# Attention stage of a four-layer graph network: a head's exponential placed behind a scaling of mid-head, its row load asked for earlier, copies of weighted sums in the buffers of x

## Chip, cores and metric

The kernel runs on one core of one Trainium2 chip. The metric is the device time in microseconds (us) of one execution; several runs of a kernel are given by their median. One further execution was taken with the hardware profiler, and all stretches below are us from the start of its span.

## The reference

Four graph layers are applied one after the other to `x` (2708 nodes by 512 features) with one symmetric 0/1 adjacency. Each layer adds its result to `x` and begins with a layer norm and a ReLU. The change lies in the third, the attention layer with 8 heads of 64 features:

```
h    = relu(layernorm(x))
Wh   = einsum('nd,hdo->hno', h, W)             # per head, 2708 x 64
e    = leaky_relu(f1[:, :, None] + f2[:, None, :], 0.2)
e    = where(adj > 0, e, -9e15)
att  = softmax(e, axis=-1)
x    = x + elu(einsum('hnm,hmo->hno', att, Wh))  # heads side by side
```

## The kernel before

**Tiling.** The 2708 nodes are cut into 22 chunks of 126 rows (the last has 62). The attention is worked as ten units: head 0 in two halves of its columns, heads 1 to 6 whole (2708 columns), head 7 in two halves. A unit has 22 steps, one for each chunk of neighbours, so there are 220 steps in one loop (L1219 to L1234). Steps are written here as m = 0 to 21 within a unit; a prime (0', 1') marks steps of the following unit.

**One step.** `make` (L876, instruction L883, VectorE) builds the weight tile `t` from the exponentiated row `rb` of the head, the column factor `ec` and the adjacency `vT`; `t` has 4 buffers. `scale` (L866, ScalarE) makes the stationary operand `whs` from `wh` (L872), and in steps that are not "by side" also its part for the sums (L874); `whs` has 4 buffers. `compare` (L894, instruction L901, ScalarE) makes a Sigmoid tile `b` (2 buffers) in the 13 "by side" steps of heads 1 to 6 (m mod 5 is 1, 3 or 4). `multiply` (L1074, matmuls L1066, TensorE) accumulates the weighted sums `av` and, in the other steps, `sums`; `multiply_sides` adds the sums of a by-side step from `b`, one step later. The loop traces `scale` and `make` three steps ahead of `multiply`, and `compare` one step ahead.

**PSUM.** There are 8 buffers of one bank each. A whole head holds five: three for `av`, two for `sums`. So the `sums` of the next head's step 0 need buffers that `evict` (L1099, copies L1105 on ScalarE into `out`, then stores on SP's queue) has to free first. `out` shares the tag `t` of pool `common` with 3 buffers.

**Row of a head.** `load_row1` (L835, DMA on SP's queue, 1.3 MB) broadcasts a head's row into `rb` (2 buffers), and `exp_row` (L845, instruction L847) takes its exponential in place on ScalarE. A buffer of `rb` is free when the last `make` of the head two before is done.

**Counting stage.** In head 0's steps 11 to 37, `mask` (L1133, copies L1138 on ScalarE) casts quarters of the adjacency into the 5 buffers of `x`, and `count_neighbors` (L1140, matmuls L1150) sums them. Four copies serve one count. Later, `load3` loads the first chunks of `x` for the work that follows the attention; these tiles use the same 5 buffers.

**What sets the order.** Each engine runs its instructions in one fixed order. It is not the order of the trace above but that of the framework's scheduler, which may place an instruction earlier as soon as its buffer is free by its own count. The dictionary `plan` (filled by `behind`) only says at which step a function is traced; `tc.issue_after(ins)` makes what is traced in its block follow `ins` on the same engine. In the scheduled program of this kernel, the exponential of head h+1 stands at the border between heads h-1 and h, directly behind the Sigmoid of step 21 and ahead of the border's copies, although it is traced in step 8 of head h; the one of head 1 runs in the middle of head 0's first half (880.93 us).

Of the kernel before, what the change touches and what calls it, by code (L numbers as in the profile page):

```python
# [8 lines left out]
F32 = mybir.dt.float32  # L9
# [5 lines left out]
AF = mybir.ActivationFunctionType  # L15
# [5 lines left out]
P = 128  # L21
# [9 lines left out]
SLOPE2 = 0.2  # L31
# [13 lines left out]
def fast_layers(  # L45
# [36 lines left out]
    nc = tc.nc  # L82
    N, D = x_in.shape
    H, _, O = w2.shape
# [7 lines left out]
    def rows(c):  # L92
        return min(R, N - c * R)
# [17 lines left out]
    XBUFS = 5  # L111
# [11 lines left out]
    common = ctx.enter_context(tc.tile_pool(name="common", bufs=2))  # L123
# [293 lines left out]
    with ExitStack() as ring_ctx:  # L417
# [30 lines left out]
        with tc.tile_pool(name="l0", bufs=2) as wk:  # L448
            units = [(g, m) for g in range(len(groups)) for m in range(NC)]
            tiles, uppers, acc, sums, xs = {}, {}, {}, {}, {}  # L450
# [352 lines left out]
    units = [(h, 0, N) for h in range(H)]  # L803
# [5 lines left out]
    def by_side(u, m):  # L809
        return 0 < units[u][0] < H - 1 and m in BY_SIDE  # L810
# [19 lines left out]
    one6 = at.tile([R, S], F32, name="one6")  # L830
    nc.gpsimd.memset(one6, 0.0)
    nc.gpsimd.memset(one6[:, 6:7], 1.0)
    row, weight, wh, whs, acc, sides, made = {}, {}, {}, {}, {}, {}, []

    def load_row1(h, lo, hi):  # L835

# [7 lines left out]

    def exp_row(h, lo, hi):  # L845
        t = row[h][:, lo:hi]
        nc.scalar.activation(t, t, AF.Exp, scale=1.0 - SLOPE2)  # L847


    GROUP = 3  # L850
# [15 lines left out]
    def scale(s):  # L866

        u, m = steps[s]
        h, q = units[u][0], rows(m)
        t = at.tile([R, O + S], F32, name="whs", bufs=4)  # L870
        by = ef[:q, m, h : h + 1]
        nc.scalar.activation(t[:q, :O], wh.pop((u, m))[:q], AF.Copy, scale=by)  # L872
        if not by_side(u, m):
            nc.scalar.activation(t[:q, O:], one6[:q], AF.Copy, scale=by)  # L874
        whs[s] = t

    def make(s):
        u, m = steps[s]
        h, lo, hi = units[u]
        q = rows(m)  # L880
        g, k = where[m]
        t = at.tile([R, N], F32, name="t2", bufs=TILES)
        ins = nc.vector.scalar_tensor_tensor(  # L883
            t[:q, : hi - lo],
            row[h][:q, lo:hi],
            ec[:q, m, h : h + 1],
            vT[g][:q, k, lo:hi],
            op0=ALU.max,
            op1=ALU.mult,
        )  # L890
        weight[s] = t
        made.append(ins.ins)
# [74 lines left out]
    def rows2(c):  # L967
        if c < LATE:
            row2(c)
        if c == EARLY - 1:  # L970
            load_row1(*units[0])

        if c == LATE:
            exps2(slice(0, EARLY))
            exp_row(*units[0])
            load_wh(0)
            load_wh(GROUP)
        if LATE < c <= LATE + 3:
            scale(len(made))
            make(len(made))  # L980
# [71 lines left out]
    def pieces(w):  # L1052

        k = -(-w // 512)
        cuts = [round(i * w / k) for i in range(k + 1)]
        return list(zip(cuts, cuts[1:]))

    def sizes_of(u):
        _, lo, hi = units[u]
        return (hi - lo) // 2, (hi - lo) // 4  # L1060
# [38 lines left out]
    def evict(u, which):  # L1099
        h, lo, hi = units[u]  # L1100
        size = sizes_of(u)[which]
        dst, height, step = (sumT, 7, S) if which else (avT, O, O)
        for p, (a, b) in zip(acc[u][which], pieces(size)):
            t = common.tile([P, D], F32, name="out", tag="t", bufs=3)
            nc.scalar.copy(t[:, : b - a], p[:, : b - a])  # L1105
            for j in range(P // step):
                nc.sync.dma_start(
                    dst[h * height : (h + 1) * height, lo + j * size + a : lo + j * size + b],
                    t[j * step : j * step + height, : b - a],
                )  # L1110
# [68 lines left out]
    def behind(s, fn, *args):  # L1179
        plan.setdefault(s, []).append((fn, args))  # L1180
# [3 lines left out]
    behind(4, exps2, slice(EARLY, NC))  # L1184
    behind(5, load_row1, *units[1])
    behind(6, exp_row, *units[1])
    behind(9, split)
    behind(30, load_l3_weights)
    behind(30, exp_nodes)
    for u in range(2, len(units)):  # L1190
        if units[u][1] == 0:
            s = max(1, u - 1) * NC
            behind(s + 4, load_row1, units[u][0], 0, N)
            behind(s + 8, exp_row, units[u][0], 0, N)
    for u in range(len(units)):
        behind((u + 1) * NC - 1, evict, u, 0)
        behind(min((u + 1) * NC, len(steps) - 1), evict, u, 1)
# [21 lines left out]
    for s in range(len(steps)):  # L1219
        if s + 6 < len(steps) and (s + 6) % NC % GROUP == 0:  # L1220
            load_wh(s + 6)
        if s + 3 < len(steps):
            scale(s + 3)
            make(s + 3)
        if s + 1 < len(steps):
            compare(s + 1)
        multiply(s)
        multiply_sides(s - 1)
        for fn, args in plan.pop(s, ()):
            if fn in (load_l3_weights, exp_nodes, split):  # L1230
                with tc.issue_after(made[s]):
                    fn(*args)
            else:
                fn(*args)  # L1234
# [698 lines left out]
def kernel(tc: tile.TileContext, *args: bass.AP):  # L1933

    nc = tc.nc
    with tc.tile_pool(name="verdict", bufs=1) as pool:
        verdict = pool.tile([1, 1], I32, name="verdict")
        fast_layers(tc, *args, verdict)
        odd = nc.values_load(verdict[0:1, 0:1], min_val=0, max_val=P + 1)
        with tc.If(odd > 0):  # L1940
            general_layers(tc, *args)
# [32 lines left out]
```

## Time and profile before

| what | value |
|---|---|
| median of 3 runs | 1825.34 us (1822.24 to 1826.04) |
| profiled execution, its own time | 1825.62 us |
| its span | 1823.8 us, so 1.8 us lie around the span |
| TensorE busy (share of span) | 1785.4 us (98%) |
| VectorE busy | 1308.3 us (72%) |
| ScalarE busy | 796.6 us (44%) |
| attention, first `av` to last `av` matmul | 856.6 to 1416 us |

How to read it: a matmul's end is modelled and matmuls overlap, so a busy TensorE does not say that it is TensorE that sets the pace. For that one has to look at one stage and see which engine has no idle time there and which engine the others wait for. The numbers after a line's bar are the busy time and the mean of one instruction in ns; what follows the second bar is idle time in front of them and what ended most of it. In a timeline the square bracket gives the idle time ahead of the line and what ended it.

### The profile page before, as it was taken

What the parts mean: (1) busy time and instruction counts of PE and PEld (TensorE: products, weight loads), DVE (VectorE), ACT (ScalarE), POOL (GpSimd) and SP (SyncE); (2) the same over time, 40 slices, a digit from 0 to 9 for tenths busy, and PEclk for the clock granted to TensorE, in tenths of its full rate; (3) what the DMA queues carried; (4) which work ended last, traced back from release to release, by engine and by line L of the source; (5) the groups of instructions that cost most, each with busy time, mean ns of one, the idle gap of its engine ahead of it and who ended that gap; (6) DMA issues with size and microseconds to landing.
All of it is one profiled execution on the core that took longest, in us unless ns stands there. A gap on an engine that the chain in (4) does not pass through costs nothing.

```text
span 1823.8 us, 30715 instructions
## 1 busy us (share of the span) xinstructions
PE 1785.4 (98%) x11884; PEld 1041.1 (57%) x11884; DVE 1308.3 (72%) x1836; ACT 796.6 (44%) x1542; POOL 245.2 (13%) x241
## 2 busy tenths in 40 slices
PE   9999999999999999999999999999999999999998
PEld 4456777654448887644544344334444445488776
DVE  4942998855446655788999999999989777533334
ACT  2632777731210000156896676776744566400000
POOL 0101323301110211266000000000000222100000
PEclk9999999999999999999999999999999999999999
DMA  7632666635462211353231121121012444313221
GB/s 247 193 112 67 204 209 199 193 80 115 116 143 58 71 57 46 94 149 104 73 89 35 33 61 41 29 61 53 15 36 53 130 139 131 95 34 109 82 68 45
DMA packets 165553, 176.62 MB, mean 97 GB/s; under 512 B 94830, under 2 KB 115792, under 8 KB 164516
## 3 DMA queue, kind: packets, MB, share of 16 engines
q1 hardware_dynamic: 143170, 131.47, 26.3%
q10 hardware_dynamic: 18484, 33.28, 5.3%
q0 software_dynamic: 3744, 9.82, 1.6%
q8 instruction: 95, 1.56, 0.4%
q14 instruction: 60, 0.49, 0.1%
HBM read 111.35 MB, written 55.15 MB: 91 GB/s over the span
## 4 chain that ended last, share of the span: by engine, by line
PE 77%; DVE 11%; DMA 5%; issue 4%; POOL 1%; ACT 1%; SPq 0%; ACTq 0%; DVEq 0%; POOLq 0%
PE acc L368 32%; PE av L1066 16%; PE nb_ps L184 6%; PE sums L1066 6%; DVE t L883 5%; PE self_ps L184 4%; PE wh_ps L184 3%; PE line_ps L184 2%; PE h_ps L184 2%; DVE cum L494 2%; PE fused_ps L312 2%; PE hT_ps L212 1%; DMA x<-x 1%; DMA rb<-rT 1%; DMA packed<-two 1%
## 5 line engine op out<-in xcount | busy, mean ns | idle before, releaser
L883 DVE SCALAR_TENSOR_TENSOR t<-rb,ec,vT 126x2708 f32<-126x2708 f32 (+2 forms) x220 | 532.4, 2469 | 20.6 <-PE sums L1066 10.9
L368 PE MATMUL acc<-halves,kt 126*126 126x512 f32 x1848 | 435.5, 395 | 3.7 <-DVE kt L741 2.1
L1066 PE MATMUL av<-t,whs 126*32 126x451 f32 (+3 forms) x4576 | 436.5, 515 | 0.6 <-DVE ln_mv L191 0.6
L368 PEld LDWEIGHTS acc<-halves,kt 126*126 126x126 f32 x1848 | 342.6, 186 | 93.1 <-DVE kt L741 6.5
L1066 PEld LDWEIGHTS av<-t,whs 126*32 126x32 f32 (+1 forms) x4576 | 160.2, 110 | 206.9 <-issue 181.7
L368 PE MATMUL acc<-halves,ar 126*126 126x512 f32 x924 | 235.4, 408 | 4.3 <-ACT ar L488 2.4
L901 ACT ACTIVATE b<-t,eb 126x2708 bf16<-126x2708 f32 (+1 forms) x78 | 199.0, 2551 | 21.2 <-DVE t L883 21.0
L368 PEld LDWEIGHTS acc<-halves,ar 126*126 126x126 f32 x924 | 171.0, 189 | 55.4 <-issue 8.1
L193 ACT ACTIVATE ln_rs<-ln_mv,eps 126x1 f32<-126x1 f32 x88 | 25.6, 293 | 341.1 <-DMA x<-x 199.2
L741 DVE SCALAR_TENSOR_TENSOR kt<-lastr,index,vT 126x504 fp32r<-126x504 int16 (+3 forms) x154 | 110.4, 728 | 80.9 <-PE acc L368 80.7
L1291 DVE CAST kt<-vT 126x504 fp32r<-126x504 uint8 (+3 forms) x154 | 55.9, 365 | 138.2 <-PE acc L368 138.2
L1066 PE MATMUL sums<-t,whs 126*32 126x338 f32 (+5 forms) x1568 | 140.5, 451 | 5.1 <-ACT out L1105 5.1
L872 ACT ACTIVATE whs<-wh,ef 126x64 f32<-126x64 f32 x220 | 76.6, 350 | 130.1 <-PE sums L1066 73.7
L1033 POOL TENSOR_SCALAR z<-y 126x512 f32<-126x512 f32 x22 | 44.0, 2000 | 664.8 <-DVE y L1026 656.0
L494 DVE TENSOR_TENSOR_SCAN cum<-ai,deg 126x504 int16<-126x504 int32 (+2 forms) x110 | 128.4, 1180 | 0.6 <-DMA ai<-in_adj 0.6
L522 ACT ACTIVATE cum<-cum,limit 126x504 int16<-126x504 int16 (+3 forms) x132 | 88.1, 667 | 59.9 <-DVE deg L502 58.9
L1066 PEld LDWEIGHTS sums<-t,whs 126*32 126x32 f32 (+1 forms) x1568 | 55.3, 109 | 73.1 <-issue 40.7
L189 DVE BATCH_NORM_STATS2 ln_st<-x 126x6 f32<-126x512 f32 x88 | 60.2, 685 | 45.7 <-DMA x<-x 30.8
L184 PE MATMUL h_ps<-w0s,hT 128*126 128x512 f32 x176 | 81.2, 605 | 4.7 <-ACT hT L214 3.5
L184 PE MATMUL nb_ps<-wfn,hT 128*126 128x512 f32 x176 | 80.7, 602 | 3.1 <-ACT hT L214 3.1
L184 PE MATMUL wh_ps<-w2s,hT 128*126 128x512 f32 (+1 forms) x176 | 79.4, 593 | 0.0
L184 PE MATMUL nb_ps<-wn,hT 128*126 128x512 f32 x176 | 79.2, 592 | 0.0
(182 smaller groups left out, 1870.6 us busy)
## 6 DMA issues: line engine op xcount, KB each, us to landing
x<-x SPq DMA_DIRECT2D x105, 252.0 KB
x<-x ACTq DMA_DIRECT2D x84, 252.0 KB
ai<-in_adj SPq DMA_DIRECT2D x84, 249.0 KB
x<-in_x SPq DMA_DIRECT2D x42, 252.0 KB
rb<-rT SPq DMA_DIRECT2D x7, 1332.8 KB
wh<-whd SPq DMA_DIRECT2D x70, 94.5 KB
packed<-two POOLq DMA_DIRECT2D x44, 124.5 KB, 4.5
whd<-wh SPq DMA_DIRECT2D x21, 252.0 KB
```

The costliest lines, as they stand in the source:

```text
L184: nc.tensor.matmul(po[:n], lhsT[:, f, :n], w[:, f, :], start=(f == 0), stop=(f == NF - 1))
L189: nc.vector.bn_stats(st[:n], xc[:n])
L368: nc.tensor.matmul(acc[:R], weight[:, k * R : (k + 1) * R], parts[:, i, :], start=(m == 0 and i == 0), stop=(m == NC - 1),)
L494: nc.vector.tensor_tensor_scan(cum[:n, :gw], ai[:n, :gw], ai[:n, :gw], 0.0 if g == 0 else deg[:n, m : m + 1], op0=ALU.add, op1=ALU.max,)
L522: nc.scalar.activation(cum[:n, :gw], cum[:n, :gw], AF.Sign, bias=limit[:n], scale=-1.0, accum_out=signs[:n, m, g : g + 1],)
L741: nc.vector.scalar_tensor_tensor(by_chunk(kt, cs), lastr[:, cs[0] * R : (cs[-1] + 1) * R].rearrange("p (c r) -> p c r", r=R), index[:R, m ...
L872: nc.scalar.activation(t[:q, :O], wh.pop((u, m))[:q], AF.Copy, scale=by)
L883: ins = nc.vector.scalar_tensor_tensor(t[:q, : hi - lo], row[h][:q, lo:hi], ec[:q, m, h : h + 1], vT[g][:q, k, lo:hi], op0=ALU.max, op1=AL ...
L901: nc.scalar.activation(b[:q, : hi - lo], weight[s][:q, : hi - lo], AF.Sigmoid, bias=eb[:q, m, h : h + 1], scale=STEEP,)
L1033: nc.gpsimd.tensor_scalar(z, y, 0.0, None, op0=ALU.min)
L1066: nc.tensor.matmul(p[j * S : (j + 1) * S, : b - a], lhsT, rhs[:, part * size + a : part * size + b], start=(s % NC == 0), stop=(s % NC == ...
L1291: nc.vector.tensor_copy(by_chunk(kt, cs), pattern(m, cs))
```

## The change

Three edits, all in the attention. First, `scale` records its instruction in a new list `scaled`, and `exp_row` is traced in a block that puts the exponential behind the last recorded scaling; it is traced in step 9 of a unit instead of 8. At that point the loop has traced `scale` up to step 12 of the unit, so it is the scaling of step 12 that the exponential now follows. Second, the row load is traced in step 2 instead of step 4. Third, copies of `av` of the six whole heads take the 5 buffers of `x` instead of the 3 of `t`; copies of `sums`, and those of the half heads, stay where they were.

```diff
     def exp_row(h, lo, hi):
         t = row[h][:, lo:hi]
-        nc.scalar.activation(t, t, AF.Exp, scale=1.0 - SLOPE2)
+        with tc.issue_after(scaled[-1]) if scaled else ExitStack():
+            nc.scalar.activation(t, t, AF.Exp, scale=1.0 - SLOPE2)
...
-        nc.scalar.activation(t[:q, :O], wh.pop((u, m))[:q], AF.Copy, scale=by)
+        ins = nc.scalar.activation(t[:q, :O], wh.pop((u, m))[:q], AF.Copy, scale=by)
         if not by_side(u, m):
             nc.scalar.activation(t[:q, O:], one6[:q], AF.Copy, scale=by)
         whs[s] = t
+        scaled.append(ins.ins)
...
         for p, (a, b) in zip(acc[u][which], pieces(size)):
-            t = common.tile([P, D], F32, name="out", tag="t", bufs=3)
+            tag, bufs = ("x", XBUFS) if (lo, hi) == (0, N) and which == 0 else ("t", 3)
+            t = common.tile([P, D], F32, name="out", tag=tag, bufs=bufs)
             nc.scalar.copy(t[:, : b - a], p[:, : b - a])
...
             s = max(1, u - 1) * NC
-            behind(s + 4, load_row1, units[u][0], 0, N)
-            behind(s + 8, exp_row, units[u][0], 0, N)
+            behind(s + 2, load_row1, units[u][0], 0, N)
+            behind(s + 9, exp_row, units[u][0], 0, N)
```

In the scheduled order this gives: on ScalarE the exponential of every head from 1 to 7 stands directly behind the scaling of step 12 of the unit ahead of it (for head 1, in head 0's second half, ahead of the four mask copies of the eleventh count). At a border, the Sigmoid of step 1' now stands ahead of the copies of `av`. On SP's queue the row loads keep their places among the other transfers; five loads of `x` move from the end of the counting stage (924 us) to behind the stores of head 6 (about 1341 us). The orders of TensorE, VectorE and GpSimd are the same.

More of the change, by code (lines that the diff above doesn't have):

```diff
@@ L832, in fast_layers @@
     nc.gpsimd.memset(one6[:, 6:7], 1.0)
-    row, weight, wh, whs, acc, sides, made = {}, {}, {}, {}, {}, {}, []
+    row, weight, wh, whs, acc, sides, made, scaled = {}, {}, {}, {}, {}, {}, [], []
     def load_row1(h, lo, hi):
```

## Prediction

> **What bounds the kernel now.** I read the page's busy shares first (TensorE 98%, which decides nothing), then the wait table for 750 to 1330 us, then VectorE alone in order of time over the attention, and last ScalarE and TensorE around the head borders. VectorE's timeline says what sets the pace in heads 1 to 6:
>
> ```profile
> 929.91 80.19 DVE L883 SCALAR_TENSOR_TENSOR t<-rb,ec,vT 126x1324 f32<-126x1324 f32 x28 [0.61 <-PE sums L1066]
> 1010.88 3.04 DVE L883 SCALAR_TENSOR_TENSOR t<-rb,ec,vT 126x2708 f32<-126x2708 f32 x1 [0.78 <-PE sums L1066]
> 1015.67 3.04 DVE L883 SCALAR_TENSOR_TENSOR t<-rb,ec,vT 126x2708 f32<-126x2708 f32 x1 [1.75 <-PE av L1066]
> 1019.03 253.81 DVE L883 SCALAR_TENSOR_TENSOR t<-rb,ec,vT 126x2708 f32<-126x2708 f32 x86 [0.31 <-PE sums L1066]
> 1273.88 3.04 DVE L883 SCALAR_TENSOR_TENSOR t<-rb,ec,vT 126x2708 f32<-126x2708 f32 x1 [1.04 <-PE sums L1066]
> 1277.43 53.39 DVE L883 SCALAR_TENSOR_TENSOR t<-rb,ec,vT 126x2708 f32<-126x2708 f32 x19 [0.51 <-ACT b L901]
> ```
>
> The columns are start, duration, instruction, and in brackets the idle time ahead of it. VectorE runs 80 us and 254 us without a gap, 253.81/86 = 2.95 us for one weight tile. TensorE needs less: the chain of waits shows 14.55 us for five steps (1024.09 to 1038.64), 2.91 us each. So a whole head costs 22 x 2.95 = 65 us of VectorE, and whatever leaves VectorE idle there is lost. It is idle at two borders, 0.78 + 1.75 + 0.31 = 2.84 us at heads 1/2 and 1.04 + 0.51 = 1.55 us at heads 5/6: **4.4 us in all**. The borders themselves, all engines in order of time:
>
> ```profile
> 998.43 2.55 ACT L901 ACTIVATE b<-t,eb 62x2708 bf16<-62x2708 f32 x1 [1.86 <-DVE t L883]
> ...
> 1001.00 1.28 ACT L847 ACT_TABLE_LOAD   x1
> ...
> 1004.95 2.46 ACT L847 ACTIVATE rb<-rb 126x2708 f32<-126x2708 f32 x1 [2.67 <-DMA rb<-rT]
> ...
> 1007.77 1.38 ACT L1105 COPY out<-av 128x451 f32<-128x451 f32 x3
> ...
> 1008.33 2.48 PE L1066 MATMUL sums<-t,whs 126*32 126x338 f32 x16 [3.41 <-ACT out L1105]
> ```
>
> ScalarE finishes the last Sigmoid, loads a table, waits 2.67 us for the row's transfer, takes the exponential, and only then copies `av`; TensorE idles 3.41 us for the freed bank. Head 0 is otherwise: there VectorE waits about 0.36 us on TensorE every second step, so TensorE sets the pace, and ScalarE has no gap between 880.93 and 927.06 us:
>
> ```profile
> 915.89 0.36 ACT L872 ACTIVATE whs<-wh,ef 126x64 f32<-126x64 f32 x1
> 916.14 0.32 ACT L874 ACTIVATE whs<-one,ef 126x32 f32<-126x32 f32 x1
> 916.35 0.76 ACT L1138 CAST x<-vT 126x677 bf16<-126x677 uint8 x1
> ...
> 917.46 2.08 ACT L1138 CAST x<-vT 126x677 bf16<-126x677 uint8 x3
> ```
>
> These are the scaling of step 12 and the four mask copies of the eleventh count. They end at 919.54 us, and TensorE's count starts at 920.17 us: 0.63 us to spare.
>
> [...] copies of banks that were long full wait behind an exponential that waits for a DMA. [...] the table of stretches grants 0.95 of the clock in 1004.5 to 1070 and 1.00 in the four neighbours, and the 16 `sums` matmuls at 1008.33 took 2.48 us where the same 16 took 1.36 at other borders. [...] at 1008.2 to 1010.7 copy, scaling, load and Sigmoid follow each other within 0.1 us.
>
> **The change part by part.**
>
> *Exponential out of the borders (gain).* At heads 1/2 call T the end of the last weight tile of head 1 (998.3). Now ScalarE has there: Sigmoid of step 21 to T+2.7, a pair of scalings to T+3.3, the Sigmoid of step 1', whose tile comes at T + 2 x 2.95 = T+5.9, to T+8.45, then the first copy (0.46) to T+8.9. TensorE wants the bank at about T+6.3 (1004.6 before) and starts at T+9.0 instead of T+10.0: it still waits, 2.7 us for 3.4. But VectorE needs that step's tile back only for the tile of step 4', at T + 4 x 2.95 = T+11.8. The `sums` now end at T+10.4 (1.36 us), before at T+12.5 (2.48 us at half clock). So VectorE doesn't wait: 2.84 us saved. At heads 5/6 the same holds and the 2.88 us wait for the row is gone: 1.55 us. At the other borders VectorE had no gap, nothing to gain. Sum **-4.4 us**.
>
> *Exponential in mid-head (nothing in heads 1 to 6).* Call V the end of the tile of step 9. ScalarE: Sigmoid 9 to V+2.55, scalings of step 12 to V+3.2, table and exponential (1.28 + 2.46) to V+6.9, scaling of 13 to V+7.25, table to V+8.55, Sigmoid 11 to V+11.1. TensorE wants that Sigmoid after step 12, at V + 8.85 + 3.42 = V+12.3, VectorE wants tile 11 back at V+14.75. What covers the 5 us are ScalarE's own waits for TensorE (67.8 us of `whs` waits in 933 to 1420). If that cover were short by more than 1.2 us, Sigmoid 11 would be late next.
>
> *Exponential of head 1 (loss).* It goes between the two scalings at 915.89 and the mask copies at 916.35: exponential to 918.8, two copies (0.69 each) to 920.2, a scaling pair to 920.7, two copies to 922.1, count at 922.2 instead of 920.17. All of TensorE is held behind the count, VectorE's four tiles are full, so its takeover at 929.9 moves by the same **+2.0 us**. Queued behind on ScalarE are the scalings of steps 13 and 14, ready at 920.7 and 922.3, wanted at 922.1 and 924.1 even without the delay; they fit. Bounds: 0 if ScalarE is ahead by then, because the old place at 880.93 is empty (it gained at most 0.11 us a pair of steps since, so I allow 0.4); 2.4 if not even the 0.63 of spare is there.
>
> *Row loads, SP's queue.* Their places among SP's transfers don't change, because they wait for the buffer of the head before last; step 2 for step 4 is worth 0. The exponential now comes some 30 us after the load is issued, for a transfer of 6.3 to 8.0 us, so its 8.9 us of DMA waits go.
>
> *Buffers of x.* The copies of `sums` waited 0.4 us once for a store; worth 0 to -0.4, taken as 0. The five moved loads of `x` (252 KB each, 0.31 us of issue each) stand among the `wh` loads of head 7. Those are issued when a buffer of three groups comes free, some 7 steps of 1.75 us = 12 us ahead of use; the row of 1333 KB took 6.3 to 8.0 us, so 1260 KB hold a `wh` back by about that: hidden. Wanted at 1402 us, issued by 1345. 0, at worst +1.
>
> Sum: -4.4 + 2.0 = **-2.4 us** on the profiled execution's 1825.62, which is 0.28 over the median: 1823.2, I say **1823.3**.
>
> **Rivals.** *The exponential in the counting stage costs nothing* (ScalarE ahead of the masks): 1825.6 - 4.4 - 0.4 = 1820.8. For it: that stage loses a 2.46 us exponential earlier. Against: the mask copies take turns with TensorE through five buffers, so ScalarE can't run ahead by more than one copy.
>
> *Slower: the clock drops in the counting stage.* A TensorE wait of 2.0 us there, with the tables full, may give a half-clock window. In a stage that TensorE sets, 3.4 to 6.8 us at half clock lose 1.7 to 3.4 us, and the remaining border wait of 2.7 us may do the same again, refilling VectorE's gap of up to 2.8. All together -4.4 + 2.0 + 3.4 + 2.8 = +3.8, and with the two later counts late by 0.5 each, +4.8: 1830. [...] against it, the 1.67 us wait at 1270.8 us left the clock at 1.00.
>
> *It does not do what it says*, the load's earlier step: shown above as worth 0 already, and the rest alone gives 1823.
>
> *Same by cancellation*: counting stage +2.0 and one drop of the clock, +1.7 to +2.8: 1825 to 1826.
>
> **How the numbers follow.** A change of 0.2% (3.65 us) is about what a measurement of this kernel can tell from none. Likeliest case 0.40 (1822 to 1824.5), cancellation 0.20, cheap counting stage 0.20, clock in both places 0.20. Faster by over 0.2% means under 1821.7: the cheap case and a little of the likeliest, less some of its own upper half: 0.20. Over 1829.0: most of the clock case, and late `x` loads on top of the cancellation: 0.20. Within: 0.60. The range of 1820.0 to 1829.2 takes in the cheap case and most of the clock case.
>
> **What would show it.** Right: no gap over 0.3 us in VectorE's run from about 932 to 1326 us; the exponential at 916 us, with a count near 922 that waits about 2 us for a mask copy; at heads 1/2 a TensorE wait near 2.7 us, ended by a copy that stands behind a Sigmoid; 30 us between a row load and its exponential. Wrong: a count at 920.2 without a wait; VectorE still idle at the borders; a granted clock under 1.00 between 916 and 935 us; `whs` waiting for a `wh` transfer in head 7.

## Result, and the profile after

| kernel | median of 17 runs each | range | profiled execution, span |
|---|---|---|---|
| before | 1825.85 us | 1821.34 to 1832.24 | 1823.8 us |
| changed | 1822.15 us | 1818.60 to 1823.74 | 1818.8 us |

The ratio of changed to before is 0.9979, with a 95% interval of 0.9971 to 0.9987. That is 3.8 us faster (2.4 to 5.3), against 2.4 us forecast. A second measurement of the changed kernel gave 0.9981 (0.9973 to 0.9989). In what follows an execution is compared with another from its first `av` matmul to its last (559.5 us before, 556.2 us after). The changed kernel's first `av` already came 2.9 us earlier, in code that the change does not touch, so that part of the two spans is not the change's.

VectorE in order of time, after the change (start, duration, instruction, idle time ahead and what ended it):

```profile
920.78 3.27 DVE L886 SCALAR_TENSOR_TENSOR t<-rb,ec,vT 126x1324 f32<-126x1324 f32 x2 [1.84 <-PE sums L1069]
...
928.33 83.14 DVE L886 SCALAR_TENSOR_TENSOR t<-rb,ec,vT 126x1324 f32<-126x1324 f32 x29 [0.64 <-PE sums L1069]
1011.63 3.04 DVE L886 SCALAR_TENSOR_TENSOR t<-rb,ec,vT 126x2708 f32<-126x2708 f32 x1 [0.16 <-PE av L1069]
1014.98 310.03 DVE L886 SCALAR_TENSOR_TENSOR t<-rb,ec,vT 126x2708 f32<-126x2708 f32 x106 [0.31 <-PE sums L1069]
1326.01 1.66 DVE L886 SCALAR_TENSOR_TENSOR t<-rb,ec,vT 126x1384 f32<-126x1384 f32 x1 [1.00 <-PE sums L1069]
```

In heads 1 to 6 only 0.16 + 0.31 us of gaps are left of 4.4; the border of heads 5/6 has vanished in a run of 106 tiles. There is a new gap of 1.84 us at 920.78, where 0.36 us is usual. It belongs to head 1's exponential in the counting stage; ScalarE and TensorE there:

```profile
912.58 0.36 ACT L874 ACTIVATE whs<-wh,ef 126x64 f32<-126x64 f32 x1
912.83 0.32 ACT L876 ACTIVATE whs<-one,ef 126x32 f32<-126x32 f32 x1
913.04 2.46 ACT L849 ACTIVATE rb<-rb 126x2708 f32<-126x2708 f32 x1
915.40 1.41 ACT L1143 CAST x<-vT 126x677 bf16<-126x677 uint8 x2
916.70 0.35 ACT L874 ACTIVATE whs<-wh,ef 126x64 f32<-126x64 f32 x1
916.95 0.32 ACT L876 ACTIVATE whs<-one,ef 126x32 f32<-126x32 f32 x1
917.16 1.41 ACT L1143 CAST x<-vT 126x677 bf16<-126x677 uint8 x2
```

```profile
917.10 0.32 PE L1155 MATMUL adj_sums<-x,parts 126*24 126x338 bf16 x2
917.97 0.30 PE L1155 MATMUL adj_sums<-x,parts 126*24 126x338 bf16 x1 [0.55 <-ACT x L1143]
918.62 0.45 PE L1155 MATMUL adj_sums<-x,parts 126*24 126x338 bf16 x5 [0.35 <-ACT x L1143]
918.77 1.41 PE L1069 MATMUL av<-t,whs 126*32 126x331 f32 x16
```

ScalarE does what was foreseen: scaling pair, exponential, two mask copies, scaling pair, two mask copies. TensorE however doesn't wait for all four copies. It starts the eight matmuls of the count in time at 917.10 and takes each quarter as it comes, with waits of 0.55 and 0.35 us. The fourth matmul needs the last copy, which ends at 918.57, and the others stand behind it. The `av` matmuls behind the count start at 918.77, 1.7 us after the count began; in the kernel before it was 0.3 us (PE there):

```profile
920.17 0.47 PE L1150 MATMUL adj_sums<-x,parts 126*24 126x338 bf16 x8
920.46 1.30 PE L1066 MATMUL av<-t,whs 126*32 126x331 f32 x16
```

So what follows the count is 1.4 us late. The border of heads 1/2, ScalarE and then TensorE:

```profile
996.84 2.55 ACT L904 ACTIVATE b<-t,eb 62x2708 bf16<-62x2708 f32 x1 [1.85 <-DVE t L886]
...
1002.71 2.55 ACT L904 ACTIVATE b<-t,eb 126x2708 bf16<-126x2708 f32 x1 [2.87 <-DVE t L886]
1005.17 1.39 ACT L1110 COPY out<-av 128x451 f32<-128x451 f32 x3
```

```profile
998.44 4.90 PE L1069 MATMUL av<-t,whs 62*32 62x451 f32 x48
1005.74 1.43 PE L1069 MATMUL sums<-t,whs 126*32 126x338 f32 x16 [2.40 <-ACT out L1110]
1007.10 0.75 PE L1069 MATMUL sums<-b,parts 62*32 62x338 bf16 x8
1007.78 5.97 PE L1069 MATMUL av<-t,whs 126*32 126x451 f32 x48
```

ScalarE stands idle for 2.87 us ahead of the Sigmoid of step 1' while the copies of the three `av` banks stand behind it, the last of which was finished at 1000.9; TensorE waits 2.40 us for the first. The 5.97 us of 48 `av` matmuls (4.7 to 4.9 elsewhere) begin in a stretch in which TensorE's granted clock was 0.50; this half clock began at 1006.9 and lasted 3.4 us.

### The profile page after: what moved, and what is told of

It reads as the page before. It is cut to its first block, busy times and chain, and to the rows that moved or that the text cites. A ratio compares the mean times of both kernels' runs of the same rounds, so it can differ in the third digit from the quotient of the medians.

```text
span 1818.8 us, 30698 instructions
## 1 busy us (share of the span) xinstructions
PE 1781.6 (98%) x11884; PEld 1036.1 (57%) x11884; DVE 1307.9 (72%) x1836; ACT 798.0 (44%) x1542; POOL 245.3 (13%) x241
## 4 chain that ended last, share of the span: by engine, by line
PE 80%; DVE 9%; issue 4%; DMA 4%; ACT 1%; POOL 1%; SPq 0%; DVEq 0%; ACTq 0%; POOLq 0%
PE acc L368 31%; PE av L1069 19%; PE nb_ps L184 7%; PE sums L1069 6%; PE self_ps L184 4%; PE wh_ps L184 3%; DVE t L886 3%; PE line_ps L184 3%; DVE cum L494 2%; PE h_ps L184 2%; PE hT_ps L212 2%; PE fused_ps L312 2%; DMA x<-x 1%; DMA ai<-in_adj 1%; DVE two L506 1%
## 5 line engine op out<-in xcount | busy, mean ns | idle before, releaser
L874 ACT ACTIVATE whs<-wh,ef 126x64 f32<-126x64 f32 x220 | 76.8, 349 | 130.6 <-PE sums L1069 66.1
```

The lines of the kernel that those rows point to most:

```text
L874: ins = nc.scalar.activation(t[:q, :O], wh.pop((u, m))[:q], AF.Copy, scale=by)
```

## Experiments

Theory A is the prediction's: the stalls of the borders go, the eleventh count pays (the expectations write tenth). Theory B says that the buffers of `x` bring the gain. Theory C came from the trace above: TensorE's remaining border wait is not free but a lag that it keeps through heads 1 to 6. The table is read from VectorE's and TensorE's timelines of each kernel's profiled execution, in us: from the first `av` to head 1's first tile, on to head 7's first tile, on to that of its second half, on to the last `av`, and their sum; and for how long the half clock stood at the border of heads 1/2. Of the second execution of before there is a profile alone. The rest can hold a later half clock: in the first profile of the changed kernel one began at 1409.7 us, 0.2 us before the last `av`.

| kernel | ratio to before (95%) | to head 1 | heads 1 to 6 | head 7a | rest | sum | half clock |
|---|---|---|---|---|---|---|---|
| before | 1 | 76.7 | 394.3 | 41.3 | 47.2 | 559.5 | 6.8 |
| before, again | | 76.6 | 391.6 | 41.3 | 47.6 | 557.1 | 0 |
| changed | 0.9979 (0.9971-0.9987) | 78.0 | 390.0 | 40.8 | 47.3 | 556.2 | 3.4 |
| changed, again | 0.9981 (0.9973-0.9989) | 78.1 | 389.4 | 40.7 | 47.2 | 555.3 | 0 |
| exponential alone | 0.9978 (0.9970-0.9986) | 78.1 | 390.1 | 40.7 | 47.2 | 556.1 | 3.4 |
| buffers of x alone | 0.9999 (0.9988-1.0010) | 76.8 | 391.7 | 41.3 | 47.7 | 557.5 | 0 |
| head 1 free | 0.9978 (0.9969-0.9986) | 76.6 | 389.4 | 40.6 | 47.2 | 553.9 | 0 |
| head 1 free, again | 0.9980 (0.9969-0.9991) | 76.9 | 390.0 | 40.7 | 48.3 | 555.9 | 3.4 |
| exponential behind copies | 0.9980 (0.9973-0.9987) | 76.6 | 389.4 | 40.7 | 48.0 | 554.6 | 0 |
| copies first | 0.9960 (0.9947-0.9973) | 78.1 | 389.4 | 37.5 | 47.2 | 552.2 | 0 |
| copies first, head 1 free | 0.9962 (0.9948-0.9975) | 76.8 | 389.4 | 37.5 | 47.2 | 550.9 | 0 |
| one more pass | 1.0006 (0.9999-1.0012) | 78.1 | 395.0 | 39.8 | 47.2 | 560.2 | 3.4 |
| three more passes | 1.0071 (1.0056-1.0086) | 78.0 | 405.6 | 40.3 | 47.2 | 571.1 | 0 |
| one more pass, copies first | 0.9965 (0.9952-0.9979) | 78.1 | 389.4 | 38.3 | 47.2 | 553.0 | 0 |

**The parts of the change.** First the exponential's placing alone (row load back at step 4, all copies in `t`):

```diff
-            behind(s + 2, load_row1, units[u][0], 0, N)
+            behind(s + 4, load_row1, units[u][0], 0, N)
...
-            tag, bufs = ("x", XBUFS) if (lo, hi) == (0, N) and which == 0 else ("t", 3)
+            tag, bufs = "t", 3
```

> The placing of the exponential alone: row load at step 4, copies in the three buffers of t. Theory A (the whole gain is the exponential out of the head borders, 4.4 us of VectorE gaps, less a later tenth count): about 1822 us, 3.5 us under the kernel before, like the changed kernel within 0.7; no gap of VectorE over 0.7 us in heads 1 to 6, the count near 921.7 us after the start of the span behind its mask copies. Theory B (the buffers of x let the border's copies start sooner, and that is where the gain comes from): under 2 us faster than before, with some 2 us of gaps left at the border of heads 1/2.

Then the kernel before with the other buffers alone:

```diff
-            t = common.tile([P, D], F32, name="out", tag="t", bufs=3)
+            tag, bufs = ("x", XBUFS) if (lo, hi) == (0, N) and which == 0 else ("t", 3)
+            t = common.tile([P, D], F32, name="out", tag=tag, bufs=bufs)
```

> The kernel before with the copies of weighted sums in the buffers of x, and nothing else. Theory A: 1825.5 us, within 0.7 us of the kernel before, VectorE's gaps of about 2.8 us at heads 1/2 unchanged. Theory B: 2 us or more faster than before.

The placing alone has the changed kernel's ratio and the changed kernel's segments to 0.1 us (its count was through by 920.6 us, where near 921.7 was expected; but the first `av` came 1.4 us earlier than before); the buffers alone have 0.9999. With `t`'s three buffers ScalarE waited six times for stores of `out`, 4.1 us in all, and nothing became later for it. B falls. The row load's step was not run alone; together with the buffers it is what separates this run from the changed kernel, and the two have the same time. One line of the buffers' run missed what A expected of it, though: VectorE's gap at heads 1/2 was 0.11 us and not 2.8, with nearly the same wait of TensorE, 3.29 us. This led to a second profile of the kernel before.

> The kernel before once more, for a second profile of it. If the 2.84 us of VectorE's gaps at heads 1/2 need the half clock that follows TensorE's wait there (a gap of 0.1 us was seen behind a wait of 3.29 us without it): first to last av is 559.5 us when the half clock is there for 6.8 us and about 557 us when it is not. The gaps of 1.3 to 1.6 us at heads 5/6 stay in either case.

TensorE at that border in this second profile of before:

```profile
1010.34 1.35 PE L1066 MATMUL sums<-t,whs 126*32 126x338 f32 x16 [3.32 <-ACT out L1105]
```

The same wait, and 1.35 us for the 16 `sums` matmuls that had taken 2.48. VectorE's gap behind it was 0.21 us; the gaps at heads 5/6 were there again (0.95 + 0.51):

```profile
1015.30 257.02 DVE L883 SCALAR_TENSOR_TENSOR t<-rb,ec,vT 126x2708 f32<-126x2708 f32 x87 [0.21 <-ACT b L901]
1273.26 3.04 DVE L883 SCALAR_TENSOR_TENSOR t<-rb,ec,vT 126x2708 f32<-126x2708 f32 x1 [0.95 <-PE sums L1066]
```

So first to last `av` is 557.1 us for 559.5. What differs is the granted clock behind the wait. The table of stretches, in pieces of 3.41 us (half of the 6.8 us at half clock in the first profile), for the first profile of before and then for its second (us, busy time of PE, PEld, DVE, ACT, POOL, then the granted clock and DMA):

```profile
1004.51:1007.93 3.42, 0.41 (x8) 0.00 (x0) 3.42 (x2) 2.98 (x4) 0.00 (x0) 1.00 0.00 0
1007.93:1011.34 3.41, 3.01 (x24) 0.73 (x24) 2.63 (x2) 3.38 (x6) 0.00 (x0) 0.50 0.57 132
```

```profile
1005.43:1008.85 3.42, 1.58 (x20) 0.28 (x11) 3.42 (x2) 1.90 (x1) 0.00 (x0) 1.00 0.14 55
1008.85:1012.26 3.41, 1.92 (x28) 0.69 (x32) 3.41 (x3) 3.39 (x8) 0.00 (x0) 1.00 0.32 75
```

Behind the wait of 3.41 us the granted clock was 0.50 for 6.8 us; behind that of 3.32 us it stayed at 1.00. The changed kernel's two profiles differ in the same way: a wait of 2.40 us was followed by 0.50 for 3.4 us, one of about 2.4 us (1.15 and 1.24 us without a matmul in two neighbouring pieces from 1006.5 us) by 1.00. So the length of the wait alone does not tell whether the clock drops. These are four executions as they fell; no run moved a wait, and what decides was not shown.

**Repeat of the changed kernel.**

> The changed kernel itself once more, beside the runs of this call: 3.7 us under the kernel before, within 1 us. Its profile shows whether the half clock at the border of heads 1/2 (3.4 us long in its first profile) is there in each execution: theory A says nothing on it; if it comes and goes, first to last av is 555.7 to 556.2 us either way.

The time is 0.9981, within what was expected, but not the segment: 555.3 us, a little shorter than either end given. This execution had no half clock at the border, and VectorE no gap at all from 933.7 us to head 7:

```profile
933.72 396.06 DVE L886 SCALAR_TENSOR_TENSOR t<-rb,ec,vT 126x1324 f32<-126x1324 f32 x136 [0.64 <-PE sums L1069]
1330.63 1.66 DVE L886 SCALAR_TENSOR_TENSOR t<-rb,ec,vT 126x1384 f32<-126x1384 f32 x1 [0.85 <-PE sums L1069]
```

So 3.4 us of half clock cost the first profile 0.6 us in heads 1 to 6, which I had not counted.

**Head 1's exponential.** It is left where it was before:

```diff
-        with tc.issue_after(scaled[-1]) if scaled else ExitStack():
+        with tc.issue_after(scaled[-1]) if scaled and h > 1 else ExitStack():
```

> The changed kernel, but the exponential of head 1 is not tied to a scaling and so goes back to its early place in head 0's first half. Theory A (the exponential in the counting stage costs what its 2.46 us leave uncovered there, 1.5 us measured, 2.0 predicted): 1820.6 us, 1.5 to 2.0 us under the changed kernel and 5 to 5.7 under the kernel before; the count back at 0.6 us or more behind its last mask copy. Rival (ScalarE has room there and the 1.5 us were something else): 1822.1 us, as the changed kernel. Theory C (TensorE's lag behind VectorE is paid at the end of head 6 only as far as it is there) asks for 1.5 us as A does.

> The changed kernel with head 1's exponential at its early place, once more, now beside the changed kernel on the same chip, because its profile was 2.2 us shorter between first and last av and its times were not. If the delay of the count is real time: 1.2 to 2.2 us under the changed kernel. If the executions that are not profiled lose it elsewhere: the same within 0.7 us.

In both profiles the stage up to head 1 is back at 76.6 and 76.9 us, the count starts in one piece and VectorE's 1.84 us gap is gone: the delay is 1.2 to 1.4 us, and it is the exponential's. The times don't show it: 0.9978 and 0.9980 beside 0.9979 and 0.9981 of the changed kernel. The intervals of two such ratios allow a gain of 1.3 us as well as none; this stays open. Executions differ by more than that in work which the change does not touch. From the last `av` to the end of the span the 14 profiles took 406.6 to 409.7 us. A half clock of 3.4 us lay in this stretch in the first profile of before (from 1427.8 us; 407.8 us in all), and one of 6.8 us began just ahead of it in the first of changed (1409.7 us; 408.9 us).

**The exponential at the border, but behind the copies.** To see whether it had to leave the border at all, the kernel before with only this:

```diff
-        nc.scalar.activation(t, t, AF.Exp, scale=1.0 - SLOPE2)
+        with tc.issue_after(copied[-1]) if h > 1 else ExitStack():
+            nc.scalar.activation(t, t, AF.Exp, scale=1.0 - SLOPE2)
...
-            nc.scalar.copy(t[:, : b - a], p[:, : b - a])
+            ins = nc.scalar.copy(t[:, : b - a], p[:, : b - a])
+            if which == 0:
+                copied.append(ins.ins)
```

> The kernel before with one edit: the exponentials of heads 2 to 7 stay at the head borders, but behind the copies of av instead of ahead of them. The wait for the row's transfer and the exponential then hold up no bank. Theory A (what cost time at a border is only that the copies stood behind the exponential): VectorE's gaps in heads 1 to 6 fall to 0.5 us or less, no delay in the counting stage, so first to last av about 554 us as in the run with head 1's exponential free, and 4 to 5.5 us under the kernel before. Rival (the exponential has to leave the border: behind the copies it makes the Sigmoids of steps 3' and 4' late, by the table loads, the wait for the transfer and its own 2.46 us): TensorE waits for b at the borders and VectorE keeps gaps of 1 us or more at some, within 2 us of the kernel before or slower.

ScalarE at its border of heads 1/2:

```profile
1006.10 1.39 ACT L1106 COPY out<-av 128x451 f32<-128x451 f32 x3
1007.37 0.36 ACT L873 ACTIVATE whs<-wh,ef 126x64 f32<-126x64 f32 x1
1007.75 1.28 ACT L848 ACT_TABLE_LOAD   x1
1009.04 2.47 ACT L848 ACTIVATE rb<-rb 126x2708 f32<-126x2708 f32 x1
```

TensorE waits 2.34 us here, VectorE has no gap in heads 1 to 6, and the ratio is 0.9980, 3.7 us: a little under what A expected in time, 554.6 us as expected in the segment, and the gain of the whole change. What cost time was the order of copies and exponential, not the exponential's place in the head.

**Copies first.** In the changed kernel, the Sigmoid of step 1' goes behind the copies of `av`:

```diff
-            nc.scalar.activation(
+            with tc.issue_after(copied[u - 1]) if m == 1 else ExitStack():
+                nc.scalar.activation(
...
-            nc.scalar.copy(t[:, : b - a], p[:, : b - a])
+            ins = nc.scalar.copy(t[:, : b - a], p[:, : b - a])
+            if which == 0:
+                copied[u] = ins.ins
```

> The changed kernel, but at each border the Sigmoid of step 1' is put behind the three copies of av, so that TensorE's bank is free some 2.4 us sooner. Theory A as predicted (TensorE's remaining border wait is hidden, because VectorE doesn't wait for it): 1822.1 us, as the changed kernel, within 0.7. Theory C (TensorE falls some 3 us behind VectorE at a border, keeps that lag through heads 1 to 6 because VectorE's four tiles take it, and pays it where head 7 is bound by TensorE): 1819 us, 2 to 3 us faster than the changed kernel, gained between the last tile of head 6 and the first tiles of head 7. In both the TensorE wait of 2.4 us at heads 1/2 and the half clock behind it are gone. Rival against both: the Sigmoid comes late for its by-side sums and a new wait of up to 1.4 us a border appears: 1824 us or more.

0.9960 from five executions, 3.5 us below the changed kernel. VectorE in order of time:

```profile
932.44 431.98 DVE L886 SCALAR_TENSOR_TENSOR t<-rb,ec,vT 126x1324 f32<-126x1324 f32 x157 [0.64 <-PE sums L1070]
```

157 tiles from head 0 to the middle of head 7 without a gap, where the changed kernel stopped for 1.00 and 1.11 us and more at the start of head 7. The whole gain lies there: head 7a takes 37.5 us for 40.7, while heads 1 to 6 need the same 389.4 us as in the changed kernel's second profile. That is theory C. TensorE's wait at a border doesn't reach VectorE, because four tiles take it up, but TensorE's lag stays until head 7 makes TensorE the slower engine, and then it is paid. Take the time from the end of VectorE's first tile of a head to TensorE's first `av` matmul with it. In the changed kernel's second profile it is 3.6 us in each of heads 3 to 6 and 4.99 us at head 7; with the copies first it falls from 0.97 to 0.50 us and is 1.88 at head 7. The difference at head 7 is the 3.1 us that head 7a gains.

TensorE's pace alone does not keep the lag. At the 2.91 us a step that the prediction read, for VectorE's 2.95, it would win 0.9 us a head; it won 0.2 us from one head to the next in the changed kernel's first profile (4.52, 4.30, 4.12 and 3.93 us in heads 3 to 6). In the second it won nothing, because at each border the copies stand behind the Sigmoid of step 1' again. ScalarE, then TensorE, at heads 2/3 of that profile:

```profile
1073.01 2.56 ACT L904 ACTIVATE b<-t,eb 126x2708 bf16<-126x2708 f32 x1 [1.40 <-DVE t L886]
1075.47 1.39 ACT L1110 COPY out<-av 128x451 f32<-128x451 f32 x3
```

```profile
1076.03 1.35 PE L1069 MATMUL sums<-t,whs 126*32 126x338 f32 x16
```

The first copy ends at about 1075.9 and the `sums` start at 1076.03. The edit acts at every border, so this run doesn't tell how much of the 3.1 us comes from heads 1/2 and how much from the later ones.

> The changed kernel with both edits of the two runs before: the exponential of head 1 back at its early place, and the Sigmoid of step 1' behind the copies of av. Theory A with C (the count's delay of 1.4 us and the lag of 3.2 us at head 6/7 are separate, so they add): first to last av matmul 550.8 us, 5.3 us less than in the changed kernel, and a time 8.5 to 9.5 us under the kernel before. Rival (one lag, paid once: with TensorE no longer behind, the count's delay is hidden too, so its removal brings nothing more): 552.2 us and 7 to 7.5 us under the kernel before, as with the copies first alone.

Both edits together have the expected 550.9 us in the profile. The time, 0.9962, is no better than with the copies first alone: again the count's delay shows in the profile and not in the times.

**How much room the mid-head has.** One more pass over the row behind the exponential, and in a second kernel three (`range(3)`); the scaling of step 13 and the Sigmoid of step 11 are tied behind them:

```diff
+            if h > 1:
+                for _ in range(1):
+                    ins = nc.scalar.copy(t, t)
+                held[h - 1] = ins.ins
...
+        with tc.issue_after(held[h]) if m == 13 and h in held else ExitStack():
...
+            with tc.issue_after(held[h]) if m == 11 and h in held else ExitStack():
```

> The changed kernel with one more pass over the row (an in-place copy, 2.4 us) directly behind the exponentials of heads 2 to 7, and the scaling of step 13 and the Sigmoid of step 11 behind it: the mid-head block of ScalarE grows from 5.0 to 7.4 us. Theory A (the block lies in slack; the Sigmoid of step 11 may end 3.65 us later before VectorE waits for its tile): VectorE keeps running without a gap in heads 1 to 6, TensorE waits up to 1.3 us in mid-head, 0 to 1 us slower than the changed kernel. Rival (ScalarE has no such slack and mid-head is bound by it): 2.4 us for each of six heads, 14 us slower.

> The same with three more passes (7.1 us): the block is 12.1 us long. Theory A: the Sigmoid of step 11 ends some 18.2 us after the tile of step 9, and VectorE wants its tile back at 14.75, so VectorE idles about 3.5 us in each of six heads: 21 us slower than the changed kernel, 18 to 24. Rival (no slack): 7.1 us for each of six heads, 43 us slower. Rival (slack is larger than worked out, since the tile is not wanted so soon): under 10 us slower.

Both miss. One pass cost 5 us (1.0006 for 0.9979) where at most 1 was expected. VectorE:

```profile
1047.53 64.98 DVE L891 SCALAR_TENSOR_TENSOR t<-rb,ec,vT 126x2708 f32<-126x2708 f32 x22 [1.67 <-ACT b L910]
1113.24 64.98 DVE L891 SCALAR_TENSOR_TENSOR t<-rb,ec,vT 126x2708 f32<-126x2708 f32 x22 [0.73 <-ACT b L910]
```

A gap in each of heads 2 to 6, ended by the Sigmoid, and none in head 1. With V the end of the tile of step 9, from the timelines of ScalarE and VectorE:

| kernel | head | exponential starts | Sigmoid 11 ends | VectorE wants the tile back |
|---|---|---|---|---|
| changed | 1 | V + 4.59 | V + 11.16 | V + 14.66 |
| changed | 2 | V + 7.29 | V + 13.85 | V + 14.66 |
| changed, again | 2 to 6 | V + 6.37 | V + 12.93 | V + 14.67 |
| one more pass | 1 | V + 4.61 | V + 13.68 | V + 14.66 |
| one more pass | 2 | V + 7.31 | V + 16.39 | V + 14.7 |
| one more pass, copies first | 1 to 6 | V + 4.6 to 4.7 | V + 13.7 to 13.8 | V + 14.67 |

In head 1 the slack is 3.5 us; in head 2 it is 0.8, because ScalarE waits for TensorE ahead of the exponential (2.57 us for a `whs` buffer in the run with one more pass), and TensorE lags from the border on. The pass makes the Sigmoid 1.7 us late in head 2, and that is the gap. With three passes the gaps add to 14 us and the run was 17 us slower than the changed kernel, under the 18 to 24 expected: in that kernel's scheduled order it is the tile of step 16, one tile of 2.95 us later, that waits for the Sigmoid (1.1 us in heads 2 to 6). The tile ahead of it waits 1.5 us for TensorE's `sums`.

> One more pass behind the exponentials of heads 2 to 7, as in the run that had it before, together with the copies of av ahead of the Sigmoid of step 1'. Theory C (it was TensorE's lag from the border that put the exponential of heads 2 to 6 some 2 to 2.7 us later after the tile of step 9, V + 6.4 to 7.3 for V + 4.6, and so used up the slack in which the pass would have lain): exponential at V + 4.6 in every head, the Sigmoid of step 11 ends at V + 13.7, a full 1 us before VectorE wants its tile, and VectorE's gaps in heads 1 to 6 stay under 1 us in all; 0 to 1.5 us slower than with the copies first alone, so about 6 us under the kernel before. Rival (the pass costs what it cost, whatever the border does): gaps of 0.7 to 1.7 us in each of heads 2 to 6, 4.5 to 5 us slower than with the copies first alone.

The expectation held: the pass that cost 5 us in the changed kernel costs 0.9 us (0.9965 for 0.9960, less than these intervals can tell from none) when TensorE has no lag, and VectorE has no gap in heads 1 to 6. The profile has 0.8 us, all of it in head 7a, 38.3 for 37.5 us. So the lag accounts for both: the slack in mid-head and the loss at head 7.

## Why the prediction was right, point by point

- **Exponential out of the borders, -4.4 us.** The mechanism was right: copies of full banks stood behind an exponential, and with that gone VectorE's gaps went. The size was that of one execution. The gaps at heads 5/6 are 1.3 to 1.6 us in all three profiles with the old placing, but the 2.84 us at heads 1/2 came with the half clock: 0.1 and 0.2 us in the two without it. From the second profile of before to the second of changed, both without half clock at the border, heads 1 to 6 gained 2.2 us; from first to first, 4.3 us.
- **Exponential of head 1, +2.0 us.** Right in place and kind, mis-sized: 1.2 to 1.4 us in the profiles. The working had the last mask copy end 1.9 us after the count was due (922.1 for 920.17); it ended 1.5 us after (918.57 for 917.10). The exponential began some 0.2 us earlier against the count than taken, and ScalarE's instructions, whose durations were added, overlap by about 0.1 us each (a scaling from 912.58 lasts 0.36, the next line starts at 912.83). The step also had the whole count wait for that copy. Three of its eight matmuls ran before it, so the sign that was named, a count near 922 us with a wait of about 2 us, did not show; but this saved only some 0.1 us.
- **TensorE's wait at the border, 2.7 us.** Measured 2.40 us, ended by a copy behind a Sigmoid. The 0.3 us are a reading: the working had TensorE want the bank at 1004.6 us, but the line that it shows puts the start of the wait at 1008.33 - 3.41 = 1004.92. "So VectorE doesn't wait" held in heads 1 to 6. That the wait is therefore worth nothing did not: it is paid at head 7, 3.1 to 3.3 us there. The sum survived this, because the kernel before paid about the same there (41.3 us for 40.7 to 40.8).
- **Exponential in mid-head, 0.** Right: the changed kernel's second profile has no gap there. The slack behind it was mis-sized: V + 11.1 was measured in head 1 (11.16), but 12.9 to 13.9 in the later heads, whose TensorE lags.
- **Row load, buffers of x, moved loads: 0.** Right. The stretch in which the moved loads of `x` lie took 47.3 and 47.2 us for 47.2 and 47.6. ScalarE's waits for the row's transfer are gone.
- **Sum, -2.4 us.** Measured -3.8 (-5.3 to -2.4). In the profiles, -1.8 us without half clock at the border in either kernel (557.1 to 555.3), -3.3 with it in both (559.5 to 556.2). Without the rest of the attention, which can hold a later half clock, the two are -1.4 and -3.4. The profile with the half clock at the border is the longer by 2.8 us of before's two, without the rest, and by 0.8 us of the changed kernel's two; how often executions without a profile meet it was not shown, so neither was its part in the measured -3.8. That -2.4 came this near, at the edge of the interval, is in part luck: 4.4 us was reached only with the half clock in both (4.3 us, and 2.2 us without), 2.0 us was too much for the loss, and the 0.5 to 0.7 us gained in head 7a was not in the sum.
- **Rivals.** The clock drop did come at the border, but at 0.6 us where 2.8 were feared, since it lasted 3.4 us where 6.8 had been seen and VectorE had tiles in hand. In the counting stage waits of 0.55 and 0.35 us left the clock alone (1.00 from 916 to 935 us).

## What to carry to other kernels

A stall seen in one profile may be a wait times a clock state (2.84 us here with half clock, 0.21 us without): look at a second profile before taking its length as what an edit saves. An engine that recovers only slowly carries a wait along, so ask not only who waits for it now but where the pace next passes to it, and what slack it has eaten in between. At the border of two accumulations, the copy that frees a bank comes first on its engine; here that order (0.9960 for 0.9979) was worth about as much again as the whole change.

## What was not expected of the hardware

The length of a wait did not tell whether TensorE's clock drops. At the border of heads 1/2 the granted clock was 0.50 for 6.8 us behind a wait of 3.41 us (first profile of before) and for 3.4 us behind one of 2.40 us (first of changed). It stayed at 1.00 behind 3.32 us (second of before) and about 2.4 us (second of changed).
